# A mixture-of-experts layer: the slot-to-token table written by scatters, bias sums and zero columns without products

## The chip, the cores and the metric

The kernel runs on one core of one Trainium2 chip. TensorE (PE) multiplies, VectorE (DVE) and ScalarE (ACT) work on elements, GpSimd (POOL) and SyncE (SP) here mostly issue DMA transfers. The metric is the device time of one launch in microseconds. The kernel before takes 1660.75 us, the median of three runs (1660.35 to 1661.57).

## The reference

The input `x` holds 2 batches of 2048 tokens with 512 features, all float32. Everything that has to be computed is this:

```python
ys  = y * scale                                       # one row of 512 per batch
d   = rsqrt(einsum('bi,io->bo', ys*ys, weight*weight) + EPS)
z   = einsum('bsi,io->bso', x * ys[:, None, :], weight) * d[:, None, :]
top1    = argmax(softmax(z @ gate_w.T))               # one of two experts per token
masked  = z[None] * one_hot(top1).T[:, :, None]       # zero rows for the other expert
routed  = (relu(masked @ w1 + b1[:, None]) @ w2 + b2[:, None]).sum(over experts)
shared  = relu(z @ sw1 + sb1) @ sw2 + sb2
out = x + routed + shared
```

A token's row is zero for the expert that it did not choose, but that expert still adds `relu(b1) @ w2 + b2` to it. So each token needs its own expert's network, the constant vector of the other expert, the shared network, and three output biases in all. The hidden width is 2048.

## The kernel before, in words

The 4096 tokens are worked on in **units** of 1024 (`U`), with features on the partitions and tokens along the free axis. Four phases follow one another on TensorE:

1. `z_unit(u)` for u = 0 to 3 makes z, stores it transposed by blocks of 128 tokens in `zD` and in features-first form in `zTD`, and collects the difference of the gate's two scores per token in `score` (`rows_of`).
2. Four shared units s0 to s3 (`unit("s0")` to `unit("s3")`), in order. Each has a layer 1 of eight steps c = 0 to 7 (`layer1_once`) and a layer 2 of seven products, each made of seven smaller ones (`layer2_twice`, places m0, m2, m3, m4).
3. Three routed units r0 to r2 of 1024 tokens and one, r3, of 512, each of one expert alone, with a small group of 128 tokens beside each of the first three.
4. A last piece of 256 tokens.

Large products are made with seven instead of eight block products, so sums and differences of weight blocks have to be made on VectorE and stored. These are the split jobs (`split_twice`), spread over the shared units; they load and store through SP's queue, which also carries all weights. The constant vector of the other expert comes out of them: `zeros_add` gathers `relu(b1)` times `w2` in a tile `part`, and `zeros_end` (L388) reduces it over partitions twice by products with ones. One gives a row of 512 (L390), stored in `zeroR`; the other gives four columns of 128 (L396), stored in `zeroC`. `begin(k)` (L1545) loads the row for the small pieces (L1558) and the column for the large ones (L1555).

Between the shared units' steps runs the **sort** (`sort_parts`, L643), a generator that is advanced one part at a time by `sort_step`. From `score` it makes for each token its position in a list of 4224 slots (`pos`), ordered by expert with padding, so that each routed piece holds one expert's tokens only. The list that the rest of the kernel needs is the inverse: the token of each slot, `idx`, with 128 partitions and 33 columns (`NS`). It is made by products with 0/1 matrices: position = 128*hi + lo, and for each block c of 128 tokens VectorE compares `lo` with a row 0 to 127 (L767) and `hi` with 0 to 32, times the token's number plus one (L768); TensorE multiplies the two into one PSUM bank `pi` that collects all 32 blocks (L759). Empty slots get a padding row (L774). The tiles of the comparisons are from the ring `io` of four buffers, which the loads of x rows use too. `idx` is used by the gathers of z rows (L1562), of the stored sums (L1654) and by the scatter of the output (L1660), all indirect DMAs on GpSimd.

The order of work is written out by hand. A dictionary `hooks` names what is to be done after a step: the places `("in", c)` and `c` of layer 1, `"m0"` to `"m4"` and `("n", step, place)` of layer 2. The sort's parts run in s0 after steps 1 to 6 and at m2, m3, m4, and in s1 and s2 after steps 5 and 6 and at m2, m3, m4.

The results of a unit leave TensorE in the next one: `run_late` takes two blocks of 128 tokens after each step c = 1 to 4 of layer 1. For each it transposes the block (L1411), adds the x row that was loaded two blocks ahead (L1505, GpSimd) on VectorE (L1508), and stores the sum in `accD` (L1509, GpSimd). GpSimd's queue also carries the loads of the next unit's z (L473). Each queue keeps its order.

Of the kernel before, what the change touches and what calls it, by code (L numbers as in the profile page):

```python
# [9 lines left out]
F32 = mybir.dt.float32  # L10
I32 = mybir.dt.int32
AF = mybir.ActivationFunctionType
ALU = mybir.AluOpType
# [3 lines left out]
def kernel(  # L17
# [9 lines left out]
    sw1: bass.AP,  # L27
    sw2: bass.AP,
    b1T: bass.AP,
    b2: bass.AP,  # L30
    out: bass.AP,
):

# [31 lines left out]
    NB = N // P  # L65
    HC = H // P
    H2 = HC // 2
# [11 lines left out]
    NS = L // P  # L79
# [3 lines left out]
    add, sub = ALU.add, ALU.subtract  # L83
# [4 lines left out]
    const = ctx.enter_context(tc.tile_pool(name="const", bufs=1))  # L88
    wpool = ctx.enter_context(tc.tile_pool(name="wpool", bufs=3))
# [32 lines left out]
    w2E = dram.tile([E, H4, P, 7, 4, P], F32, name="w2E")  # L122

    zeroR = dram.tile([E, D], F32, name="zeroR")
    zeroC = dram.tile([E, P, KD], F32, name="zeroC")


    cond_sb = const.tile([P, KD, B], F32, name="cond_sb")
# [12 lines left out]
    ones = const.tile([P, P], F32, name="ones")  # L141
# [9 lines left out]
    nc.sync.dma_start(xt[0][:, :K2, T:], xT_v[:, :K2, T:U])  # L151
    nc.scalar.dma_start(xt[0][:, K2:, T:], xT_v[:, K2:, T:U])
    b1_sb = const.tile([P, E + 1, HC], F32, name="b1_sb")
    b2_sb = wpool.tile([P, D], F32, tag="w1b", name="b2_sb")
    gate_sb = wpool.tile([P, E, D], F32, tag="w1a", name="gate_sb")

    def later_loads():

        nc.scalar.dma_start(b2_sb[: E + 1, :], b2)
        load_xT(1, nc.scalar)  # L160
        nc.scalar.dma_start(gate_sb, gate.unsqueeze(0).to_broadcast([P, E, D]))
        nc.scalar.dma_start(b1_sb, b1T.rearrange("e p c -> p e c"))
# [26 lines left out]
    col_f = const.tile([P, P], F32, name="col_f")  # L189
    nc.vector.tensor_copy(col_f, col_i)  # L190

    pad_f = const.tile([P, 1], F32, name="pad_f")
    nc.vector.tensor_scalar(pad_f, tok_f[:, :1], float(N + 1), None, add)

    def sums(o, a11, a12, a21, a22):
        s1, s2, s3, s4 = o
# [33 lines left out]
    def modulation_parts():  # L230
        for k in range(KD):
            nc.scalar.activation(cw2[:, k, :], cw_sb[:, k, :], AF.Square)
        var = const.tile([P, KD, B], F32, name="var")
        pd = bank("pa", "pd")
        for k in range(KD):
            nc.tensor.matmul(pd[:B, :D], ys2[:, k, :], cw2[:, k, :], start=(k == 0), stop=(k == KD - 1))
        vr = work.tile([P, D], F32, tag="zrow", name="vr", bufs=2)
        nc.vector.tensor_scalar_add(vr[:B, :], pd[:B, :D], EPS)
        yield
        pv = bank("pa", "pv")  # L240
        for o in range(KD):
# [12 lines left out]
        yield  # L254

        pb = bank("pa", "pb")
        for o in range(KD):
            nc.tensor.matmul(
                pb[:, o : o + 1], b2_sb[: E + 1, ts(o, P)], ones[: E + 1, :1], start=True, stop=True
            )  # L260
        nc.vector.tensor_copy(bsum, pb[:, :KD])
        yield

    modulation = modulation_parts()
# [123 lines left out]
    def zeros_end(e):  # L388
        pc = bank("pa", f"pcr{e}")
        nc.tensor.matmul(pc[:1, :D], ones[:, :1], part[e], start=True, stop=True)  # L390
        row = io(f"crow{e}")
        nc.vector.tensor_copy(row[:1, :], pc[:1, :D])
        nc.gpsimd.dma_start(zeroR[1 - e].unsqueeze(0), row[:1, :])
        pc = bank("pa", f"pcc{e}")
        for o in range(KD):
            nc.tensor.matmul(pc[:, o : o + 1], part[e][:, ts(o, P)], ones[:, :1], start=True, stop=True)  # L396
        col = const.tile([P, KD], F32, name=f"ccol{e}")
        nc.vector.tensor_copy(col, pc[:, :KD])
        nc.gpsimd.dma_start(zeroC[1 - e], col)

    split_jobs = [job_w2(sw2, q, w2S[0], s2S[0], None) for q in range(H4)]
    split_jobs += [job_w1(e, q) for e in range(E) for q in range(H4)]
# [237 lines left out]
    def small(name, shape=None, dtype=F32):  # L640
        return const.tile(shape or [P, 1], dtype, name=name)

    def sort_parts():  # L643
# [101 lines left out]
        hi = small("hi", [P, NB])  # L745
        nc.vector.tensor_sub(hi, pos, lo)
        nc.vector.tensor_scalar_mul(hi, hi, 1.0 / P)
        tok1 = small("tok1", [P, NB])
        nc.vector.tensor_scalar(tok1, tok_f, 1.0, None, add)
        yield  # L750


        pi = bank("po", "pi")
        G = 4
        for c0 in range(0, NB + G, G):
            if c0 > 0:
                for i in range(G):
                    c = c0 - G + i
                    nc.tensor.matmul(  # L759
                        pi[:, :NS], at_lo[:, i], at_hi[:, i], start=(c == 0), stop=(c == NB - 1)  # L760
                    )
            if c0 < NB:
                at_lo = io(f"at_lo{c0}", [P, G, P])
                at_hi = io(f"at_hi{c0}", [P, G, NS])
                for i in range(G):
                    c = c0 + i
                    nc.vector.tensor_scalar(at_lo[:, i], col_f, lo[:, c : c + 1], None, ALU.is_equal)  # L767
                    nc.vector.tensor_scalar(  # L768
                        at_hi[:, i], col_f[:, :NS], hi[:, c : c + 1], tok1[:, c : c + 1],
                        ALU.is_equal, ALU.mult,  # L770
                    )
                yield
        none = small("none", [P, NS])
        nc.vector.tensor_scalar(none, pi[:, :NS], 0.0, pad_f, ALU.is_equal, ALU.mult)  # L774
        idx_f = small("idx_f", [P, NS])
        nc.vector.scalar_tensor_tensor(idx_f, pi[:, :NS], -1.0, none, add, add)
        idx = small("idx", [P, NS], I32)
        nc.vector.tensor_copy(idx, idx_f)
        box["idx"] = idx
        yield  # L780

# [763 lines left out]
    def begin(k):  # L1545

        ev = nc.values_load(
            box["tab"][:, k : k + 1], engines=(mybir.EngineType.SP,), min_val=0, max_val=E - 1,
            skip_runtime_bounds_check_because="a comparison's result, 0 or 1",
        )  # L1550
        b1p = work.tile([P, HC], F32, tag="b1p", name=f"b1p{k}", bufs=3)
        nc.sync.dma_start(b1p, b1T[bass.ds(ev, 1), :, :].rearrange("e p c -> p (e c)"))
        if pieces[k][1] >= T:
            zero = work.tile([P, KD], F32, tag="zc", name=f"zc{k}", bufs=2)
            nc.sync.dma_start(zero, zeroC[bass.ds(ev, 1)].rearrange("e p k -> p (e k)"))  # L1555
        else:
            zero = work.tile([P, D], F32, tag="zrow", name=f"zrow{k}", bufs=2)
            nc.sync.dma_start(zero, zeroR[bass.ds(ev, 1), :].to_broadcast([P, D]))  # L1558
        return ev, b1p, zero
# [153 lines left out]
    box["ws"] = [(w, lambda: None) for w, _ in first]  # L1713
    for u in range(NU):
        hooks = split_hooks(5, 2 if u == 0 else 1)
        if u < 3:
            when = range(1 if u == 0 else H2 - 3, H2 - 1)
            hooks = merge(hooks, {c: [sort_step] for c in [*when, "m2", "m3", "m4"]})
        if u == 0:
            hooks = merge(hooks, {  # L1720
                ("in", 0): [lambda: [rows_of(NU - 1, j) for j in range(3)]],
                0: [lambda: [rows_of(NU - 1, j) for j in range(3, 6)]],
                ("in", 1): [lambda: [rows_of(NU - 1, j) for j in range(6, U // P)]],
            })
# [112 lines left out]
```

## Time and profile before

| what | value |
|---|---|
| median of three runs | 1660.75 us (1660.35 to 1661.57) |
| the profiled execution | 1662.84 us |
| its span | 1661.1 us |
| TensorE busy | 1645.4 us, 99% |
| VectorE busy | 1109.1 us, 67% |
| ScalarE busy | 558.5 us, 34% |
| GpSimd busy | 189.9 us, 11% |
| moved by DMA | 366.07 MB, mean 220 GB/s |

The profile shows one execution. Busy times are unions of the instructions' times of one engine, so overlapping instructions count once. PE is the matmul itself, PEld its weight load, which runs beside other matmuls; a float32 matmul of the program stands as two records of each. In the order of time a row gives the start, the length, engine, line, operation and tiles, the count of merged instructions, and in square brackets the idle time before it with what ended it. L numbers are lines of the kernel before.

In time, the shared units stand as follows: s1 begins at 303 us, s2 at 493, s3 at 683, and the routed units begin at 875 us.

### The profile page before, as it was taken

The page shows a single profiled execution, that of the slowest core. Times are in us where ns is not written, and L with a number is a line of the kernel's source. Part 1 is how long each engine was busy: PE and PEld are TensorE (multiplying, and loading weights), DVE is VectorE, ACT ScalarE, POOL GpSimd, SP SyncE. Part 2 cuts the span into 40 slices and gives each one's busy share as a digit, 9 for nine tenths or more (in the row PEclk, how much of TensorE's full clock was granted, in tenths as well). Part 3 has the DMA queues.
Part 4 walks back from the last instruction along what each step waited for, and adds up shares of the span by engine and source line. Part 5 has one row for each costly group of instructions (what it writes and reads, how often), then busy time and mean ns, then how long its engine had stood idle before and what let it go on. Part 6 is the DMA issues. An engine that isn't in the chain of part 4 may idle for free. (4 is left out here: it accounts for less than half of the span.)

```text
span 1661.1 us, 19807 instructions
## 1 busy us (share of the span) xinstructions
PE 1645.4 (99%) x6786; PEld 1203.9 (72%) x6786; DVE 1109.1 (67%) x1823; ACT 558.5 (34%) x1090; POOL 189.9 (11%) x252
## 2 busy tenths in 40 slices
PE   9999999999999999999999999999999999999997
PEld 4444478645884468644888888888888888888884
DVE  5676978676877868596855588655886558874310
ACT  3334421244113331234224363243722447224210
POOL 1221000010001000011100012011110121002210
PEclk9999999999999999999999999999999999999999
DMA  5768955998578945989565665657566575544661
GB/s 180 282 238 302 361 164 175 288 351 276 165 231 287 353 145 160 301 304 332 154 208 185 236 201 185 210 180 240 188 191 209 189 237 179 164 138 143 212 229 44
DMA packets 287368, 366.07 MB, mean 220 GB/s; under 512 B 18403, under 2 KB 218595, under 8 KB 287270
## 3 DMA queue, kind: packets, MB, share of 16 engines
q1 hardware_dynamic: 263040, 287.44, 53.1%
q0 software_dynamic: 21536, 73.16, 12.4%
q10 hardware_dynamic: 2694, 4.23, 0.7%
q8 instruction: 54, 0.88, 0.2%
q14 instruction: 44, 0.36, 0.1%
HBM read 265.92 MB, written 98.84 MB: 220 GB/s over the span
## 5 line engine op out<-in xcount | busy, mean ns | idle before, releaser
L863 PE MATMUL p1s<-zs_all,was 128*128 128x512 f32 x288 | 136.0, 597 | 1.9 <-DMA was<-sw 1.9
L1312 PE MATMUL a11s<-zs_all,w2s 128*128 128x256 f32 x416 | 97.8, 379 | 0.0
L863 PEld LDWEIGHTS p1s<-zs_all,was 128*128 128x128 f32 x288 | 53.2, 190 | 60.3 <-issue 56.0
L863 PE MATMUL p1s<-zs_all,wbs 128*128 128x512 f32 x192 | 89.2, 592 | 0.0
L1312 PEld LDWEIGHTS a11s<-zs_all,w2s 128*128 128x128 f32 x416 | 78.9, 190 | 10.6
L1660 POOL DMA_INDIRECT out<-ar,idx x33 | 34.2, 1036 | 434.7 <-DVE ar L1659 414.3
L1025 PE MATMUL a11r<-tr,war 128*128 128x256 f32 x288 | 74.4, 381 | 0.3
L1312 PE MATMUL a11r<-zs_all,w2r 128*128 128x256 f32 x312 | 73.7, 379 | 0.0
L863 PEld LDWEIGHTS p1s<-zs_all,wbs 128*128 128x128 f32 x192 | 36.4, 190 | 46.1 <-issue 43.8
L1312 PEld LDWEIGHTS a11r<-zs_all,w2r 128*128 128x128 f32 x312 | 58.8, 190 | 7.7
L1025 PEld LDWEIGHTS a11r<-tr,war 128*128 128x128 f32 x288 | 54.2, 190 | 9.2 <-ACT u2r L1056 1.5
L896 DVE TENSOR_TENSOR h1s<-p5s,u3s 128x512 f32<-128x512 f32 x32 | 22.0, 689 | 47.0 <-ACT u3s L893 35.8
L1654 POOL DMA_INDIRECT ar<-accD,idx x33 | 36.5, 1106 | 147.7 <-PE pst L1572 135.3
L1312 PE MATMUL S1s<-zs_all,w2s 128*128 128x256 f32 x224 | 52.9, 379 | 0.0
L908 DVE TENSOR_TENSOR h3s<-p5s,u2s 128x512 f32<-128x512 f32 x32 | 21.9, 686 | 43.0 <-PE p5s L863 43.0
L870 ACT ACTIVATE h2s<-p1s,b_sb 128x512 f32<-128x512 f32 x32 | 22.0, 688 | 78.6 <-PE p1s L863 78.6
L1474 PEld LDWEIGHTS phr<-zp,ws 128*128 128x128 f32 x384 | 46.2, 192 | 0.9
L473 POOL DMA_DIRECT2D zs_all<-zTD x16 | 11.5, 730 | 308.6 <-PE S1s L1312 225.0
L1312 PEld LDWEIGHTS S1s<-zs_all,w2s 128*128 128x128 f32 x224 | 42.6, 190 | 5.8
L1474 PE MATMUL phr<-zp,ws 128*128 128x128 f32 x384 | 46.8, 275 | 0.0
L870 ACT ACTIVATE h0s<-p1s,b_sb 128x512 f32<-128x512 f32 x32 | 22.0, 687 | 73.5 <-PE p1s L863 73.5
L863 PE MATMUL p5s<-zs_all,was 128*128 128x512 f32 x96 | 46.2, 604 | 0.0
(484 smaller groups left out, 3839.1 us busy)
## 6 DMA issues: line engine op xcount, KB each, us to landing
ws<-w SPq DMA_DIRECT2D x48, 512.0 KB, 6.1
w2s<-w2S SPq DMA_DIRECT2D x28, 768.0 KB, 5.0
war<-w1E SPq DMA_DIRECT2D x42, 512.0 KB, 5.1
wbr<-w1E SPq DMA_DIRECT2D x42, 384.0 KB, 3.7
w2r<-w2E SPq DMA_DIRECT2D x21, 768.0 KB, 5.2
w2r<-s2E SPq DMA_DIRECT2D x20, 512.0 KB, 3.6
was<-s1S SPq DMA_DIRECT2D x24, 384.0 KB, 6.3
zTD<-zt POOLq DMA_DIRECT2D x8, 1024.0 KB, 5.2
```

The costliest lines, as they stand in the source:

```text
L473: nc.gpsimd.dma_start(zslot(slot), zTD[u][:, k : k + K2, t : t + T])
L863: nc.tensor.matmul(ps, self.w[l][:, k, :], zslot(zi, W)[:, k, :], start=(start and k == 0), stop=(k == K2 - 1), skip_group_check=not start,)
L870: nc.scalar.activation(o, i, AF.Relu, bias=bias[:, hc : hc + 1], scale=1.0)
L896: nc.vector.tensor_add(h22[:, self.c, :], self.b5, self.u3)
L908: nc.vector.tensor_add(h12[:, self.c, :], self.b5, self.u2)
L1025: nc.tensor.matmul(halves_of(ps)[:, i], w[:, i, k % 4], self.x.of[m], start=(start and i == 0), stop=True, skip_group_check=True,)
L1312: nc.tensor.matmul(ps, self.w[m][:, c, :], self.x.of[m][:, c, :], start=(start and c == 0), stop=(c == H4 - 1), skip_group_check=not start,)
L1474: nc.tensor.matmul(ph[:, ts(i, P)], w[:, k * W + i * P : k * W + (i + 1) * P], zt[:, k, :], start=(k == 0), stop=(k == KD - 1),)
L1654: nc.gpsimd.indirect_dma_start(out=ar, out_offset=None, in_=accD[:, :], in_offset=at)
L1660: nc.gpsimd.indirect_dma_start(out=out[:, :], out_offset=at, in_=ar, in_offset=None)
```

## The change

Three things are made another way.

The table `idx` is no longer a product. A table `tokD` of 4224 entries in DRAM is filled with the padding rows by one plain write, from an `idx` that starts as padding (one iota instruction). Then, for each block of 128 tokens, one indirect DMA on GpSimd writes the 128 token numbers, 4 bytes each, to their places lo*33 + hi. At the end one plain read brings the table back as `idx`. The 32 scatters are placed in layer 1 of s1 and s2, two to a step (`("in", c)` and `c`), 16 in each unit; the read is at m2 of s2. The parts of the sort ahead of that stay in s0, up to m2.

The sum of the three output biases is a reduction on VectorE over a tile that is loaded with features on the partitions, where it was four products with ones.

The zero column is not made or stored; `begin` reads the row vector of `zeroR` in column order, 4 bytes at a time.

```diff
-    zeroC = dram.tile([E, P, KD], F32, name="zeroC")
-    b2_sb = wpool.tile([P, D], F32, tag="w1b", name="b2_sb")
+    b2_sb = const.tile([P, KD, E + 1], F32, name="b2_sb")
-        nc.scalar.dma_start(b2_sb[: E + 1, :], b2)
+        nc.scalar.dma_start(b2_sb, b2T)
+    tokD = dram.tile([P * NS, 1], I32, name="tokD")
+    idx = const.tile([P, NS], I32, name="idx")
+    nc.gpsimd.iota(idx, pattern=[[0, NS]], base=N, channel_multiplier=1)
...
-        pb = bank("pa", "pb")
-        for o in range(KD):
-            nc.tensor.matmul(
-                pb[:, o : o + 1], b2_sb[: E + 1, ts(o, P)], ones[: E + 1, :1], start=True, stop=True
-            )
-        nc.vector.tensor_copy(bsum, pb[:, :KD])
+        nc.vector.reduce_sum(bsum, b2_sb, axis=mybir.AxisListType.X)
...
-        pc = bank("pa", f"pcc{e}")
-        for o in range(KD):
-            nc.tensor.matmul(pc[:, o : o + 1], part[e][:, ts(o, P)], ones[:, :1], start=True, stop=True)
-        col = const.tile([P, KD], F32, name=f"ccol{e}")
-        nc.vector.tensor_copy(col, pc[:, :KD])
-        nc.gpsimd.dma_start(zeroC[1 - e], col)
...
-        tok1 = small("tok1", [P, NB])
-        nc.vector.tensor_scalar(tok1, tok_f, 1.0, None, add)
+        at_f = small("at_f", [P, NB])
+        nc.vector.scalar_tensor_tensor(at_f, lo, float(NS), hi, ALU.mult, add)
+        at_i = small("at_i", [P, NB], I32)
+        nc.vector.tensor_copy(at_i, at_f)
+        table = tokD.rearrange("(p c) o -> p (c o)", c=NS)
+        nc.gpsimd.dma_start(table, idx)
         yield
-        pi = bank("po", "pi")
-        G = 4
-        for c0 in range(0, NB + G, G):
-            if c0 > 0:
-                for i in range(G):
-                    c = c0 - G + i
-                    nc.tensor.matmul(
-                        pi[:, :NS], at_lo[:, i], at_hi[:, i], start=(c == 0), stop=(c == NB - 1)
-                    )
-            if c0 < NB:
-                at_lo = io(f"at_lo{c0}", [P, G, P])
-                at_hi = io(f"at_hi{c0}", [P, G, NS])
-                for i in range(G):
-                    c = c0 + i
-                    nc.vector.tensor_scalar(at_lo[:, i], col_f, lo[:, c : c + 1], None, ALU.is_equal)
-                    nc.vector.tensor_scalar(
-                        at_hi[:, i], col_f[:, :NS], hi[:, c : c + 1], tok1[:, c : c + 1],
-                        ALU.is_equal, ALU.mult,
-                    )
-                yield
...
+        for c in range(NB):
+            nc.gpsimd.indirect_dma_start(
+                out=tokD[:, :], out_offset=bass.IndirectOffsetOnAxis(ap=at_i[:, c : c + 1], axis=0),
+                in_=tok_i[:, c : c + 1], in_offset=None,
+            )
+            yield
+        nc.gpsimd.dma_start(idx, table)
...
-            nc.sync.dma_start(zero, zeroC[bass.ds(ev, 1)].rearrange("e p k -> p (e k)"))
+            nc.sync.dma_start(zero, zeroR[bass.ds(ev, 1), :].rearrange("e (k p) -> p (e k)", p=P))
...
-        if u < 3:
-            when = range(1 if u == 0 else H2 - 3, H2 - 1)
-            hooks = merge(hooks, {c: [sort_step] for c in [*when, "m2", "m3", "m4"]})
+        if u == 0:
+            hooks = merge(hooks, {c: [sort_step] for c in [*range(1, H2 - 1), "m2"]})
+        elif u < 3:
+            hooks = merge(hooks, {k: [sort_step] for c in range(H2) for k in (("in", c), c)})
+        if u == 2:
+            hooks = merge(hooks, {"m2": [sort_step]})
```

More of the change, by code (lines that the diff above doesn't have):

```diff
@@ L29 @@
     b1T: bass.AP,
-    b2: bass.AP,
+    b2T: bass.AP,
     out: bass.AP,
@@ L190 @@
     nc.vector.tensor_copy(col_f, col_i)
-    pad_f = const.tile([P, 1], F32, name="pad_f")
-    nc.vector.tensor_scalar(pad_f, tok_f[:, :1], float(N + 1), None, add)
+    tokD = dram.tile([P * NS, 1], I32, name="tokD")
+    idx = const.tile([P, NS], I32, name="idx")
+    nc.gpsimd.iota(idx, pattern=[[0, NS]], base=N, channel_multiplier=1)
     def sums(o, a11, a12, a21, a22):
@@ L747, in sort_parts @@
         nc.vector.tensor_scalar_mul(hi, hi, 1.0 / P)
-        tok1 = small("tok1", [P, NB])
-        nc.vector.tensor_scalar(tok1, tok_f, 1.0, None, add)
-        yield
-        pi = bank("po", "pi")
-        G = 4
-        for c0 in range(0, NB + G, G):
-            if c0 > 0:
-                for i in range(G):
-                    c = c0 - G + i
-                    nc.tensor.matmul(
-                        pi[:, :NS], at_lo[:, i], at_hi[:, i], start=(c == 0), stop=(c == NB - 1)
-                    )
-            if c0 < NB:
-                at_lo = io(f"at_lo{c0}", [P, G, P])
-                at_hi = io(f"at_hi{c0}", [P, G, NS])
-                for i in range(G):
-                    c = c0 + i
-                    nc.vector.tensor_scalar(at_lo[:, i], col_f, lo[:, c : c + 1], None, ALU.is_equal)
-                    nc.vector.tensor_scalar(
-                        at_hi[:, i], col_f[:, :NS], hi[:, c : c + 1], tok1[:, c : c + 1],
-                        ALU.is_equal, ALU.mult,
-                    )
-                yield
[L773 to L778, printed above, removed]
+        at_f = small("at_f", [P, NB])
[4 more added lines that the diff above has]
+        nc.gpsimd.dma_start(table, idx)
+        yield
+        for c in range(NB):
[5 more added lines that the diff above has]
+        nc.gpsimd.dma_start(idx, table)
         box["idx"] = idx
@@ L1821 @@
         ("b1T", b1.reshape(E + 1, H // P, P).transpose(0, 2, 1)),
-        ("b2", b2),
+        ("b2T", rows_to_partitions(b2)),
     ]
```

## The prediction

> **What bounds the kernel now.** I read the page's engine shares and slices first, then the groups by shape, then the order of time around the instructions that go, and last the GpSimd queue, because that is where the work goes to. The span is 1661.1 us and its execution took 1662.84 us, so 1.7 us lie around the span; the median of the runs shown, 1660.75 us, is 2.1 us below that execution. I take differences from the profile and subtract them from the median.
>
> ```profile
> span 1661.1 us, 19807 instructions
> ...
> PE 1645.4 (99%) x6786; PEld 1203.9 (72%) x6786; DVE 1109.1 (67%) x1823; ACT 558.5 (34%) x1090; POOL 189.9 (11%) x252
> ...
> DMA  5768955998578945989565665657566575544661
> ```
>
> TensorE is busy 99% of the span, so a microsecond taken off it is a microsecond off the time, unless a wait opens in its place. The DMA row shows where one could: slices at 8 and 9 tenths lie in the shared units. The groups by shape (line, engine, operation, tiles, shape, count, then busy us and mean ns) show what the change takes off TensorE:
>
> ```profile
> L759 PE MATMUL pi<-at_hi,at_lo 128*128 128x33 f32 x64 | 7.8, 266 | 0.0
> ...
> L396 PE MATMUL pcc<-ones,part 128*128 128x1 f32 x16 | 2.1, 253 | 0.0
> ...
> L258 PE MATMUL pb<-ones,b_sb 3*128 3x1 f32 x8 | 1.0, 248 | 0.0
> ```
>
> The busy sums overlap at their edges, so I take starts instead. In the order of time (start, us, engine, line) one of the eight L759 groups, at the seam of units s1 and s2, is:
>
> ```profile
> 490.39 1.89 PE L1312 MATMUL a11s<-zs_all,w2s 128*128 128x256 f32 x8
> 492.12 0.98 PE L759 MATMUL pi<-at_hi,at_lo 128*128 128x33 f32 x8
> 492.93 1.96 PE L863 MATMUL p1s<-zs_all,was 128*128 128x512 f32 x4
> ```
>
> From the first product of L759 to the next useful product: 492.93 - 492.12 = 0.81 us, with no gap before or after. Does the neighbour close up when the group goes? The seam of s2 and s3 is the same code without it:
>
> ```profile
> 681.16 1.89 PE L1312 MATMUL a11s<-zs_all,w2s 128*128 128x256 f32 x8
> 682.88 1.88 PE L863 MATMUL p1s<-zs_all,was 128*128 128x512 f32 x4
> ```
>
> There the next unit begins 1.72 us after the eight records of L1312 began, their own length, and no wait follows. So the 0.81 us is really paid and nothing behind it is waiting to take its place.
>
> **What the change takes away.** (1) The 32 placement products: 8 groups of 0.81 us = 6.48 us. (2) The four bias products, L258: 28.59 us to 29.57 us, 0.98 us. The reduction that replaces them is one VectorE instruction (a reduction at L677 took 186 ns, the removed copy 161 ns) and no longer waits for TensorE. What follows on TensorE then starts 1 us earlier; its fourth product needs VectorE's L542, which ended at 31.0 us and starts earlier too, while that product moves from 33.1 to 32.1 us, so no wait opens. (3) The column products of the two zero vectors, L396: 714.00 to 714.92 us, and 771.89 to 772.80 us, together 1.83 us. Sum: 6.48 + 0.98 + 1.83 = **9.3 us**.
>
> Here a rule can be set beside the row. The Trainium skill, page "TensorE: Matmul & The Clock Gate", section "Wait — 56ns, not 53.3ns?", gives a small matmul a floor of about 25 ns from start to start, or about 62 ns where the sequencer's code handles it. By the second, 88 records (64 + 8 + 16) would cost 5.5 us, by the first 2.2 us. The row says 0.81 us for eight, about 101 ns each: each record has a 190 ns weight load of its own, and these follow one another. I use the row.
>
> VectorE loses 64 comparisons and some small ones; the comparisons start 0.2 us apart, so 13 us go. I cost that at nothing: VectorE is busy 67%, and TensorE's waits for it are already under half a microsecond. The two instructions that make the scatter's addresses are of the size of L749's (174 ns) and stand in for it.
>
> **What it adds.** In the compiled order the GpSimd queue gains one table write, 32 scatters and one read, and loses two column stores. TensorE gains nothing. Each scatter waits until the one before it has landed, and behind a waiting scatter stand, in this order, the stores of finished sums (L1509) and the loads of x rows (L1505); VectorE's L1508 waits for those loads, and behind it the sums that free TensorE's banks. In units s1 and s2 the queue holds three scatters ahead of the first stores, two for each later group of two blocks, and seven after the last group. The queue now, unit s2:
>
> ```profile
> 517.75 1.14 POOL L1509 DMA_DIRECT2D accD<-xr  x2 [23.26 <-DVE xr L1508]
> 520.35 0.54 POOL L1505 DMA_DIRECT2D xr<-x  x1 [1.45 <-DMA accD<-xr]
> 521.50 0.54 POOL L1505 DMA_DIRECT2D xr<-x  x1 [0.61 <-DMA accD<-xr]
> 530.64 1.15 POOL L1509 DMA_DIRECT2D accD<-xr  x2 [8.60 <-DVE xr L1508]
> ```
>
> One group takes 530.64 - 517.75 = 12.9 us, of which the queue works 2.2. A scatter's issue is bounded by the indirect stores L1660 (979 ns at least, 990 median, 1692 most); I take 1.0. Its landing time L has no row; the nearest is the small column store on the same queue:
>
> ```profile
> L399 POOL DMA_DIRECT2D zeroC<-ccol x2: 564/569/574, 715.6 to 773.8; - x2
> ...
> DMA to landing us min/median/max: 1.7/4.4/7.0
> ```
>
> and above it the x loads, which a scatter stands behind: 3.0 least, 5.7 median, 8.4 most. The Trainium skill speaks against this part of the change: "DMA: Bandwidth & Descriptors", section "Anatomy of one DMA — SWDGE (gpsimd) path", makes about 2.0 us of every GpSimd DMA a fixed cost, most of it the receipt of the write; a chain of 32 pays it 32 times. By that rule L is 2.0 us, by the rows 4.4 to 8.4 us. Per group the queue then needs 2.2 (stores and loads) + 1.0 + L + 1.0 = 4.2 + L: 6.2 us by the rule, 8.6 by the median, 12.6 by the longest. All are below 12.9, so the queue keeps pace. The three early scatters, at most 3 x 9.4 = 28 us, begin when the x loads are out; at seam s1 that is about 294 us (the comparisons' buffers that held those loads back until 304.7 are gone) and the first store is not due until 329.0. The seven late ones (at most 66 us) come ahead of the next unit's loads of z (L473), of which the first goes out at 631.5 us, 71 us after the last store of s2 at 560.2, and serves the seam at 683. So I cost the scatters at nothing for TensorE; if that cover is gone, see the rival below.
>
> The x loads now also go out directly behind the stores instead of after their landing, because the placement tiles no longer share their ring of four. The zero column is read from the row vector in 512 pieces of 4 bytes, four times, on the SP queue. The packet records show 9 ns for a 4-byte packet: 512 x 9 / 16 = 0.3 us; by the column load's own row it lands in 3.9 to 7.0 us. Its value is first used by L1272 at 1059.5 us, issued at 780.9, and SP's wait for the column store, 5.2 us at 775.6 us, goes or shrinks. The bias load is still 6 KB, at 10.6 us for use at 28.6. Nothing for each of these.
>
> **What stays uncertain.** One real wait for weights exists, in unit s2, in the order of time:
>
> ```profile
> 556.97 2.63 PE L863 MATMUL p1s<-zs_all,was 128*128 128x512 f32 x4 [1.91 <-DMA was<-sw]
> ```
>
> The DMA engines are full there; the window's row has stretch, length, busy PE, PEld, DVE, ACT, POOL, then clock, DMA share, GB/s:
>
> ```profile
> 540.00:560.00 20.00, 18.09 (x53) 8.65 (x52) 14.73 (x31) 7.38 (x13) 3.11 (x6) 0.95 1.03 390
> ```
>
> The wait itself is 2.1 us against the usual start-to-start, and the five slow products behind it, with the clock at 0.95 in this window, add 1.7: 3.8 us. Moved x loads can dissolve this wait or make another one. I keep it, with plus and minus 3.8.
>
> **The rivals.**
> A, the forecast: 9.3 us go, nothing replaces them: 1660.75 - 9.3 = **1651.4 us**. Its own range 1650 to 1653.5. Chance 0.62.
> B, the weight wait goes too: 1651.4 - 3.8 = 1647.6 us. For it: the x loads leave the full stretch earlier. Against: the bytes are the same. 0.12.
> C, one more such wait: 1655.2 us, two: 1659. For it: stores and loads now come in one burst of 1 MB. Against: unit s3 issues them that way already (stores at 707.62, loads at 708.76 us) and shows no such wait. 0.14.
> D, the change does not do what it says: products go, but the chains behind them (VectorE's and ScalarE's) set the pace at these seams, and half the gain stays: 1656 us. Against: the s2-s3 seam. 0.06.
> E, slower: the scatter chain backs up in s1 and s2. It begins when L exceeds 8.7 us. The queue is then late by 2(L - 8.7) when it issues the last x loads; they have 12.9 - 2.2 - 5.7 = 5.0 us to spare. Two units lose 2 x (2(L - 8.7) - 5.0), which eats the 9.3 us at L = 13.5. At L = 16 it is 19 us: 1670.6 us. Nothing the page shows on this queue for so few bytes is near it; the full DMA engines speak for it. 0.06.
>
> **How the numbers follow.** A measurement of this kernel tells about 0.2%, 3.3 us, from no change. Below 1657.4 lie A, B, D and most of C: faster 0.90. Between 1657.4 and 1664.1 lies C with two waits and the mild end of E: same 0.05. Slower 0.05. The range holds A, B, D and C with one wait and leaves out two waits and E: 1647 to 1657.5.
>
> **What would show it.** TensorE's busy time falls by 9 to 10 us to about 1636 us, with 88 fewer records, and no line waits on it for more than now. The seam at s1-s2 looks like the one at s2-s3. The scatters land in 2 to 8 us, the stores L1509 still wait for VectorE, never VectorE's L1508 for a load. A wrong prediction would show as L1508 waiting for x loads, or as TensorE waiting for weights at more places than the one in s2.

## The result and the profile after

| what | before | after |
|---|---|---|
| median | 1660.75 us (1659.34 to 1663.51, 21 runs) | 1658.47 us (1654.85 to 1660.62, 21 runs) |
| ratio of after to before | | 0.9984 [0.9977, 0.9990] |
| the profiled execution | 1662.84 us | 1657.31 us |
| its span | 1661.1 us | 1655.5 us |
| last product of TensorE ends | 1652.8 us | 1644.4 us |
| from there to the end of the span | 8.3 us | 11.1 us |

The change took off 2.3 us by the medians, 0.14%, where 9.3 us were forecast. The gain is clear of zero (the ratio's interval ends at 0.9990), but it is smaller than the 3.3 us that the prediction takes for telling a difference, and the time is 1.0 us above the upper end of its range. The removal itself went as forecast. The page of the kernel after:

```profile
span 1655.5 us, 19595 instructions
...
PE 1636.8 (99%) x6698; PEld 1194.3 (72%) x6698; DVE 1095.6 (66%) x1754; ACT 558.3 (34%) x1090; POOL 226.0 (14%) x285
...
DMA  5768955998579945898565656656566575545660
```

There are 88 records fewer and 8.6 us less of PE, where 9 to 10 were predicted. The order of time at the seam of s1 and s2 (start, us, engine, line; L1284 was L1312 and L835 was L863) shows no trace of the placement products, and nothing in their place:

```profile
486.30 1.89 PE L1284 MATMUL a11s<-zs_all,w2s 128*128 128x256 f32 x8
488.03 1.88 PE L835 MATMUL p1s<-zs_all,was 128*128 128x512 f32 x4
```

The distance is 1.73 us, that of the seam of s2 and s3 before. The gain was given back in two other places. The first is the end of the kernel. The line of the program's last instructions, L1832 before and L1807 after, has this row for GpSimd's queue (least, median and greatest duration in ns, first and last start):

```profile
L1832 POOLq DRAIN  x3: 46/109/6617, 1653.6 to 1660.8; - x3
```

and in the kernel after:

```profile
L1807 POOLq DRAIN  x3: 46/109/9132, 1645.2 to 1655.2; - x3
```

The drains stand behind an engine's last work. The longest of GpSimd's three begins as its last DMA goes out, after TensorE's last product, with no work of TensorE left that could cover it. It took 6.6 us before and takes 9.1 us now: 2.5 of the 2.8 us by which the end grew. The transfer isn't what it waits for: SyncE's wait for the landing of `out` ended 7.2 us before the end of the span in the kernel after (4.4 us before).

The second place is in s1 and s2, where TensorE waits for weights. In the order of time, at step c = 5 of layer 1 in s1, before:

```profile
365.31 1.04 PE L1411 MATMUL pos<-ident,os 128*128 128x128 f32 x8
366.19 1.88 PE L863 MATMUL p1s<-zs_all,was 128*128 128x512 f32 x4
```

and at this step of s1 and of s2, after:

```profile
363.31 1.04 PE L1383 MATMUL pos<-ident,os 128*128 128x128 f32 x8
365.24 1.95 PE L835 MATMUL p1s<-zs_all,was 128*128 128x512 f32 x4 [0.90 <-DMA was<-sw]
...
549.04 1.04 PE L1383 MATMUL pos<-ident,os 128*128 128x128 f32 x8
552.13 2.75 PE L835 MATMUL p1s<-zs_all,was 128*128 128x512 f32 x4 [2.05 <-DMA was<-sw]
554.68 2.82 PE L835 MATMUL p5s<-zs_all,was 128*128 128x512 f32 x4
```

The wait in s2 is the old one (1.91 us in the prediction's line of before); the one in s1 is not in the execution of before. To count them I add up, over s1 and s2, by how much the distance between two products exceeds the usual one; the slow products behind a long wait (2.82 us for four in place of 1.88) are in that sum. The profiled execution of before has 0 us in s1 and 3.8 in s2, that of after 1.3 and 3.8. But these are single executions, and the one of before happened to lie 2.1 us above its median, the one of after 1.2 us below. Brought to the medians (the sum plus the median less the execution, which takes it that the executions of a kernel differ in these waits alone), before has 3.8 - 2.1 = 1.7 us and after 5.1 + 1.2 = 6.3 us. So, as an estimate, the waits add 4.6 us, and the account for the medians is -9.3 + 2.8 + 4.6 = -1.9 us, against -2.3 measured.

### The profile page after: what moved, and what is told of

Same layout as the page of the kernel before. It is cut to its first block, busy times and chain, and to the rows that moved or that the text cites. A ratio compares the mean times of both kernels' runs of the same rounds, so it can differ in the third digit from the quotient of the medians.

```text
span 1655.5 us, 19595 instructions
## 1 busy us (share of the span) xinstructions
PE 1636.8 (99%) x6698; PEld 1194.3 (72%) x6698; DVE 1095.6 (66%) x1754; ACT 558.3 (34%) x1090; POOL 226.0 (14%) x285
## 5 line engine op out<-in xcount | busy, mean ns | idle before, releaser
L835 PE MATMUL p1s<-zs_all,was 128*128 128x512 f32 x288 | 135.3, 596 | 3.1 <-DMA was<-sw 2.9
L835 PEld LDWEIGHTS p1s<-zs_all,was 128*128 128x128 f32 x288 | 53.6, 190 | 64.9 <-issue 63.0
L1284 PE MATMUL a11s<-zs_all,w2s 128*128 128x256 f32 x416 | 97.8, 379 | 0.0
L835 PE MATMUL p1s<-zs_all,wbs 128*128 128x512 f32 x192 | 89.2, 592 | 0.0
L1284 PEld LDWEIGHTS a11s<-zs_all,w2s 128*128 128x128 f32 x416 | 78.9, 190 | 10.6
L1284 PE MATMUL a11r<-zs_all,w2r 128*128 128x256 f32 x312 | 73.7, 379 | 0.0
L835 PEld LDWEIGHTS p1s<-zs_all,wbs 128*128 128x128 f32 x192 | 36.4, 190 | 46.0 <-issue 44.2
L1284 PEld LDWEIGHTS a11r<-zs_all,w2r 128*128 128x128 f32 x312 | 58.8, 190 | 7.7
L1284 PE MATMUL S1s<-zs_all,w2s 128*128 128x256 f32 x224 | 52.9, 379 | 0.0
L745 POOL DMA_INDIRECT tokD<-tok_i,at_i x32 | 36.0, 1125 | 107.5 <-DMA tokD<-tok_i,at_i 98.2
L1284 PEld LDWEIGHTS S1s<-zs_all,w2s 128*128 128x128 f32 x224 | 42.6, 190 | 5.8
L835 PE MATMUL p5s<-zs_all,was 128*128 128x512 f32 x96 | 46.0, 603 | 0.0
```

Of the source, the lines that this page charges most:

```text
L745: nc.gpsimd.indirect_dma_start(out=tokD[:, :], out_offset=bass.IndirectOffsetOnAxis(ap=at_i[:, c : c + 1], axis=0), in_=tok_i[:, c : c + 1 ...
L835: nc.tensor.matmul(ps, self.w[l][:, k, :], zslot(zi, W)[:, k, :], start=(start and k == 0), stop=(k == K2 - 1), skip_group_check=not start,)
L1284: nc.tensor.matmul(ps, self.w[m][:, c, :], self.x.of[m][:, c, :], start=(start and c == 0), stop=(c == H4 - 1), skip_group_check=not start,)
```

## The experiments

Two questions: does the drain explain the end, and what of the change makes the waits? The first theory had two parts, R for the ring of four x tiles (x loads go out directly behind the stores, because the placement tiles no longer share it) and S for the scatters in the full stretch of layer 1. The rivals were N, that TensorE now comes sooner to a stretch that the DMA engines limit, and that the drain only absorbs a landing that would be waited for anyway. "Waits" below are the sums just described, in s1 and s2 of the profiled execution.

### One part alone: bias sums and zero columns

The kernel before, with only these parts of the change (the two column stores of GpSimd go with them, so 240 of its 242 DMAs are left):

```diff
...
-            nc.tensor.matmul(
-                pb[:, o : o + 1], b2_sb[: E + 1, ts(o, P)], ones[: E + 1, :1], start=True, stop=True
-            )
-        nc.vector.tensor_copy(bsum, pb[:, :KD])
+        nc.vector.reduce_sum(bsum, b2_sb, axis=mybir.AxisListType.X)
...
-            nc.tensor.matmul(pc[:, o : o + 1], part[e][:, ts(o, P)], ones[:, :1], start=True, stop=True)
...
-            nc.sync.dma_start(zero, zeroC[bass.ds(ev, 1)].rearrange("e p k -> p (e k)"))
+            nc.sync.dma_start(zero, zeroR[bass.ds(ev, 1), :].rearrange("e (k p) -> p (e k)", p=P))
```

> The kernel before with two of the three parts of the change: the bias sums and the zero columns without products; the table is still made by products, so GpSimd gets no scatter. Theory (the drain that ends GpSimd's queue grows with its indirect DMAs, and waits for weights are added in s1 and s2 by the table's part alone): the 2.8 us of the removed products come off in full, 1658.0 us, GpSimd's last drain stays at 6.6 us. Rival (every removed product in front of the DMA-bound units is given back there as a wait for weights): the 1.0 us of the bias is given back, at most 1.8 us come off, 1659 us.

1657.17 us against 1660.26 us, ratio 0.9979 [0.9972, 0.9986]: 3.1 us less, between 2.3 and 4.6. The last drain took 6.45 us, and s1 had no wait. The 24 small records are worth what their row said, 2.8 us, and these two parts give nothing back. By the floor of 62 ns in the Trainium skill ("TensorE: Matmul & The Clock Gate", "Wait — 56ns, not 53.3ns?") they would have been worth 1.5 us, which the interval leaves out.

### The ring held as it was

Two of the four tiles of the ring are taken at m4 of the unit before and given back at step 5, as the placement tiles did; no product comes back.

```diff
...
+    def hold_two():
+        for i in range(2):
+            t = io(f"hold{i}_{len(held_io)}")
+            nc.vector.memset(t[:, :1], 0.0)
+            held_io.append(t)
+    def let_go():
+        for i in range(2):
+            nc.vector.tensor_copy(seen[:, i : i + 1], held_io.pop(0)[:, :1])
...
+        if u < 2:
+            hooks = merge(hooks, {"m4": [hold_two]})
+        if 0 < u < 3:
+            hooks = merge(hooks, {5: [let_go]})
```

> The changed kernel, but two of the four buffers of the ring io are held through steps 0 to 4 of s1 and s2, as the comparison tiles held them in the kernel before, so the loads of x rows wait again for the landing of the stores. Theory R (the bunched stores and loads add the waits for weights): the added waits go, some 4 us come off against the changed kernel's 1658.5, about 1654.5 us, no wait for weights in s1. Rival S (the scatters themselves add them) and rival N (TensorE reaches a stretch that the DMA engines limit): no difference, 1658.5 us. The drain stays at 9.1 us in all.

1655.83 us, ratio 0.9972 [0.9963, 0.9981]: 4.4 us less than before, 2.1 more than the change itself took off, where theory R forecast some 4. The intervals of the two kernels are about 1.5 and 1 us wide to each side, so this gain alone is barely clear of noise. The wait in s1 is 0.2 us. In s2 its profiled execution has 6.2 us, but that execution, 1658.86 us, is nearly its slowest. The drain is 9.13 us as in the kernel after.

### The scatters moved to layer 2

They leave layer 1: in s1 and s2 one goes behind each of 16 smaller products of layer 2. `gate` makes one half of the addresses at m0, so that no scatter is issued ahead of it.

```diff
...
-            hooks = merge(hooks, {k: [sort_step] for c in range(H2) for k in (("in", c), c)})
+            hooks = merge(hooks, {"m0": [gate]})
+            places = [("n", s, n) for s in (3, 2, 5) for n in range(1, 8)][:NB // 2]
+            hooks = merge(hooks, {k: [sort_step] for k in places})
         if u == 2:
-            hooks = merge(hooks, {"m2": [sort_step]})
+            hooks = merge(hooks, {("n", 7, 7): [sort_step]})
```

> The changed kernel with all 32 scatters moved out of layer 1 into layer 2 of s1 and s2 (16 each, held back by a copy of their addresses on VectorE at m0), where the DMA engines are half idle. Theory S (scatters in the full stretch slow the weights): about 4 us come off, 1654.5 us. Rivals R and N: no difference, 1658.5 us. The drain stays at 9.1 us, as the number of indirect DMAs is the same.

1657.63 us, ratio 0.9981 [0.9972, 0.9990], 2.6 us less than before: as good as the kernel after, where theory S forecast 4 us better. The wait in s1 is still there (1.2 us), the drain too (9.13 us). So the scatters' place alone is not what costs.

### Without the scatters

This kernel leaves out the 32 table writes, so that its gathers read the padding row and its output is not the reference's. All else stays.

```diff
         for c in range(NB):
-            nc.gpsimd.indirect_dma_start(
-                out=tokD[:, :], out_offset=bass.IndirectOffsetOnAxis(ap=at_i[:, c : c + 1], axis=0),
-                in_=tok_i[:, c : c + 1], in_offset=None,
-            )
             yield
```

> The changed kernel without its 32 scatters: the table keeps its padding rows, so every gather reads padding and the output is not the reference's; all other instructions are the same. Theory (the drain grows by 79 ns for each indirect DMA): the last drain is 6.6 us again, 2.5 us come off by it, 1656.0 us if S is wrong, about 1651.5 if S is right as well. Rival (the drain's length is chance or goes with the time): it stays at 9.1 us.

1653.33 us, ratio 0.9965 [0.9952, 0.9977], 6.9 us less than before, with a last drain of 6.53 us. That lies between its two forecasts. So by the medians the 32 scatters cost 4.6 us together: 2.6 in the drain, which the rows show, and 2.0 by the difference, which is within the noise of these medians. The wait at step 5 of s1 is there without them (2.0 us in s1), so it does not need the scatters. It stands in all five executions profiled with a free ring (0.8 to 1.5 us idle), and in none of the three with two tiles held. But the ring is not its only cause: among the kernels built on the kernel before, where the placement tiles share the ring, the last one below, with 64 loads more, idles 1.0 us at the same place.

### The drain ahead of time, in the kernel before

If the last drain pays for DMAs long landed, one drain where GpSimd has nothing to do should shorten it. The edit puts one behind the last two gathers, more than 30 us ahead of GpSimd's next DMA.

```diff
-        late.append(lambda: lambda: layer2(*prev, [after(j) for j in range(n // P)]))
+        def last():
+            thens = [after(j) for j in range(n // P)]
+            nc.gpsimd.drain()
+            layer2(*prev, thens)
+        late.append(lambda: last)
```

> The kernel before with one drain instruction more in GpSimd's queue, behind the last two gathers of sums, where the queue is idle for over 30 us. Theory (GpSimd's last drain has work to do for every indirect DMA since the last drain): the drain in the middle takes 6 us or more beside TensorE's last products, the last one falls from 6.6 to about 3 us, which is what the landing of the last store takes, and 3.5 us come off: 1656.8 us. Rival (the last drain's length is fixed by what is on the chip at the end, or counts all since the start): no change, 1660.3 us.

1657.25 us, ratio 0.9982 [0.9975, 0.9989]: one instruction makes the kernel before 3.0 us faster. The rows of the new drain and of the last ones:

```profile
L1458 POOLq DRAIN  x1: 8055/8055/8055, 1613.4 to 1613.4; - x1
```

```profile
L1837 POOLq DRAIN  x3: 46/109/3112, 1652.7 to 1656.6; - x3
```

The 8.1 us now lie beside TensorE's work, and the last drain is 3.5 us shorter. A drain's row begins while DMAs ahead of it in the queue are still to be issued: 2.8 us of the new drain pass until the two gathers are out, and 1.2 us of each last drain until the last store is. The rival, that the time at the end is the landing of the last store, falls: that store stayed.

### The same drain in the kernel after

The edit is the one above.

> The changed kernel with nothing but one drain more in GpSimd's queue, behind the last two gathers of sums. Theory: the last drain falls from 9.1 to 3.1 us, 6.0 us come off the changed kernel, 1652.6 us; the waits for weights in s1 and s2 stay. Rival (drain and waits are coupled): another time.

1653.29 us, ratio 0.9960 [0.9948, 0.9971]: 7.2 us less than before, 4.9 less than the change alone. From TensorE's end to the end of the span it is now 5.0 us. The waits stay: 2.4 and 4.0 us. So the drain costs by itself, whatever the waits do.

### The ring held and the scatters in layer 2

Both edits of above, no drain.

> The changed kernel with both moves of the single tests: two buffers of the ring held as in the kernel before, and the 32 scatters in layer 2. It is the best kernel so far without its drain in the middle. Theory (the held ring and the scatters' place each take waits for weights away, the drain stays at 9.1 us): 1646.6 + 6.0 = 1652.6 us, waits in s1 and s2 under 1 us. Rival (the drain in the middle takes the waits of s2 away in some way of its own): 1655 us or more, with a wait of 2 to 6 us in s2.

1652.34 us, ratio 0.9952 [0.9939, 0.9965], 8.1 us less than before. In the order of time at the two places:

```profile
362.94 1.04 PE L1383 MATMUL pos<-ident,os 128*128 128x128 f32 x8
363.81 1.88 PE L835 MATMUL p1s<-zs_all,was 128*128 128x512 f32 x4
...
547.47 1.04 PE L1383 MATMUL pos<-ident,os 128*128 128x128 f32 x8
548.34 1.88 PE L835 MATMUL p1s<-zs_all,was 128*128 128x512 f32 x4
```

Both waits are gone: the next product begins 0.87 us after the eight small ones, their own length. The four kernels with the same drain of 9.1 us stand like this (difference of the median to the kernel before measured beside it):

| | scatters in layer 1 | scatters in layer 2 |
|---|---|---|
| ring free | -2.3 us (the change), -1.7 in its second measurement | -2.6 us |
| ring held | -4.4 us | -8.1 us |

Moving the scatters alone gains 0.3 to 0.9 us on the change, holding the ring alone 2.1 to 2.7, both together 5.8 to 6.4. The last is well clear of noise; that it is more than the sum of the other two is not, by these medians. The traces point the same way: with either move alone a wait is left in s2 (6.2 us with the ring held, 1.6 with the scatters moved), with both there is none.

### All three

> The changed kernel with three things of the experiments: two buffers of the ring held through steps 0 to 4 of s1 and s2, the scatters in layer 2, and a drain in the middle of the last piece. Theory (all of the loss is drain and added waits for weights): 1660.3 - 9.3 - 3.5 = 1647.5 us, with the usual wait of s2 left. If the drain can't be moved, 1653.5; if the waits come back in another place, up to 4 us more.

1646.62 us, ratio 0.9917 [0.9903, 0.9931]: 13.7 us less than before, the fastest of all, 11.9 below the kernel after. Its drains:

```profile
L1430 POOLq DRAIN  x1: 10572/10572/10572, 1602.4 to 1602.4; - x1
```

```profile
L1839 POOLq DRAIN  x3: 46/109/3087, 1640.7 to 1644.6; - x3
```

The account closes here: -9.3 for the products, 5.0 us at the end in place of 8.3 (-3.3), and waits of 0.9 us in place of 1.7 (-0.8) make -13.4.

### The change once more

The kernel after without an edit, measured beside the drain in the kernel before.

> The changed kernel as it is, once more, beside these runs and on the same chip. Theory (the wait in s1 comes from the free ring): a wait for weights of 1 to 2 us at step 5 of s1 again, one of 1.4 to 6 us in s2, drain 9.1 us, 1658 us. Rival (the wait in s1 was chance): none in s1.

1658.59 us, ratio 0.9987 [0.9980, 0.9993]; drain 9.13 us, waits 1.8 and 4.4 us. The result, the long drain and both waits repeat.

### What the drain counts: 64 small stores

Is it only indirect DMAs that lengthen it? Stores of 128 x 4 bytes to spare tables, 16 in a row in each shared unit, were put in the kernel before.

```diff
+    spareD = [dram.tile([P, 1], F32, name=f"spareD{i}") for i in range(8)]
+    def plain():
+        for i in range(16):
+            nc.gpsimd.dma_start(spareD[i % 8], tok_f[:, :1])
...
+        hooks = merge(hooks, {("n", 3, 4): [plain]})
```

> The kernel before with 64 small plain stores more on GpSimd's queue (128 x 4 bytes each, 16 at a time in layer 2 of every shared unit), which nothing reads. Theory (only indirect DMAs lengthen the drain): 6.6 us. Rival (every DMA of GpSimd lengthens it by 79 ns): 11.6 us.

Both sides missed: one execution took 1841.23 us, 181 us more, with a last drain of 4.09 us. The page of that run has, in the groups and among the DMA issues (count, size of each, us to landing):

```profile
L863 PE MATMUL p1s<-zs_all,was 128*128 128x512 f32 x288 | 142.5, 621 | 68.5 <-DMA was<-sw 68.5
```

```profile
spareD<-tok_f POOLq DMA_DIRECT2D x64, 0.5 KB, 27.5
```

Stores of half a KB take 27.5 us to land in the median, and TensorE waits 68.5 us for weights in this group alone. While the stores of s0 are under way, the DMA engines are busy and move next to nothing; the same window (stretch, length, busy PE, PEld, DVE, ACT and POOL, clock, DMA share, GB/s) in the kernel before and in this one:

```profile
210.00:220.00 10.00, 10.00 (x24) 4.49 (x24) 1.60 (x3) 4.40 (x8) 0.00 (x0) 1.00 1.06 318
```

```profile
210.00:220.00 10.00, 10.00 (x25) 4.43 (x24) 2.02 (x8) 4.98 (x9) 0.00 (x0) 1.00 1.22 19
```

What holds the engines was not shown, and a kernel so disturbed could not answer the question.

### 32 plain loads

Loads of 128 x 132 bytes, each behind the landing of the one before, in layer 2 of s1 and s2 of the kernel before; nothing uses what they load.

```diff
...
+    def plain():
+        nc.vector.memset(spare, 0.0)
+        for i in range(16):
+            nc.gpsimd.dma_start(spare, x[ts(i, P), :NS])
...
+        if 0 < u < 3:
+            hooks = merge(hooks, {"m0": [plain]})
```

> The kernel before with 32 small plain loads more on GpSimd's queue (128 rows of 132 bytes, one waiting for the other, 16 each in layer 2 of s1 and s2), which nothing reads. The 64 plain stores left a last drain of 4.1 us, which fits neither a drain of indirect DMAs alone (6.6) nor one that grows for good (11.6). Theory (the drain clears up what GpSimd has issued since some earlier clearing, of whatever kind, 80 ns each): 6.6 + 2.6 = 9.2 us. Rival (plain DMAs don't count or shorten it): 6.6 us or less.

1662.84 us in one execution, 1660.44 us for the kernel before beside it, and the drain

```profile
L1841 POOLq DRAIN  x3: 46/109/9145, 1651.1 to 1660.8; - x3
```

is that of 32 scatters within 20 ns. Up to this number, what counts is how many DMAs GpSimd issues, not their kind: 242 of them gave 6.5 to 6.6 us, 274 gave 9.1, in four kernels with scatters and in this one. That is 2.5 us for 32, about 80 ns each.

### 64 plain loads

The same loads in all four shared units. If the drain grows straight on, it is 11.7 us; if the short drain of the 64 stores had to do with their number, it is 4 us again.

```diff
-        if 0 < u < 3:
+        if u < 4:
             hooks = merge(hooks, {"m0": [plain]})
```

> The kernel before with 64 chained plain loads of 128 x 132 bytes on the GpSimd queue, 16 in layer 2 of each of s0 to s3, into a tile that nothing uses. The last GpSimd drain took 6.6 us with none of them, 9.1 us with 32, and 4.1 us in the kernel with 64 plain stores. Theory, the drain grows straight with the number of GpSimd DMAs: 6.6 + 64 x 0.08 = 11.7 us. Rival, something clears the account once the number passes some point between 274 and 306 DMAs: about 4 us again, as with the 64 stores, and then what counts is the DMAs since the last clearing, not their total. The time itself should stay within 6 us of the kernel before.

```profile
L1841 POOLq DRAIN  x3: 51/109/4086, 1651.8 to 1656.4; - x3
```

4.09 us, as with the stores. So the drain does not grow with the total: something seems to clear the account on the way. The order of time on GpSimd shows a candidate. Its rows end with the idle time before the DMA and what ended it; `issue` stands for a wait that the profile puts down to nothing:

```profile
807.56 0.54 POOL L1718 DMA_DIRECT2D spare<-x  x1 [4.20 <-DMA spare<-x]
813.75 0.53 POOL L1718 DMA_DIRECT2D spare<-x  x1 [5.66 <-issue]
```

The load that the second one waits for had landed at 811.1 us by the trace's semaphore records. It goes out 2.65 us later, where the others of this chain follow a landing by 0.3 us in the median. Counted from the start of the kernel, 181 DMAs of GpSimd lie ahead of that pause. Another one, of 1.8 us, stands behind the first 84. In the kernel after the place behind the first 84 falls on a scatter:

```profile
342.47 1.03 POOL L745 DMA_INDIRECT tokD<-tok_i,at_i  x1 [0.30 <-issue]
350.47 1.01 POOL L745 DMA_INDIRECT tokD<-tok_i,at_i  x1 [6.96 <-issue]
```

Most of the 6.96 us is the landing of the scatter before (at 349.1 us); the pause behind it is 1.4 us, again in place of 0.3. A pause behind 84 shows in every run whose next DMA was ready then, seven in all. The one behind 181 does not: in the kernel before and in that of 64 stores the DMA there goes out 0.3 us after the one before it, without a pause.

If the account were cleared at 84 and 181, which are 97 apart, the next place would be 278, between the 274 DMAs of the kernel after and the 306 here. Then 59, 61, 93 and 28 DMAs would remain for the last drain in the kernels with 240, 242, 274 and 306, and 1.9 us + 78 ns for each gives 6.5, 6.7, 9.2 and 4.1 us; measured are 6.45, 6.5 to 6.6, 9.1 and 4.1. That is a guess that fits, no more: two constants and three places for four lengths, no pause to be seen at 278, where GpSimd waits for other engines, and none at 181 in other kernels. After an explicit drain with two DMAs behind it the line would give 2.1 us and 2.8 to 3.1 were measured, so it doesn't hold down to the smallest counts. What is shown is that the drain gets short again somewhere between 274 and 306.

From TensorE's last product to the end of the span this kernel takes 5.8 us, 2.5 less than the kernel before. Its one execution took 1658.45 us and that of the kernel before beside it 1661.26; that says nothing, since the 21 runs of the kernel before lie 4.2 us apart.

## Why the prediction was off

**The removal sum was right.** 9.3 us for 88 records held up: the records are gone, PE is busy 8.6 us less although products behind the waits run slower, the seam closed up, unit s3 is shorter by 1.78 us (its zero columns were put at 1.83), and the bias and zero parts alone gave 3.1 us. Row against floor went to the row. The reason that was given for the row does not hold: the 190 ns weight loads cannot follow one another within 101 ns, and in the trace they start 0.11 us apart and overlap. What sets the 101 to 115 ns of a small record was not shown.

**The scatters do keep pace.** Rival E is out. They took 969 to 2007 ns to issue, 1014 in the median, where 1.0 was taken:

```profile
L745 POOL DMA_INDIRECT tokD<-tok_i,at_i x32: 969/1014/2007, 294.5 to 588.5; - x32
...
  DMA tokD<-tok_i,at_i: 98.2, 23
```

The second line is the idle time in front of scatters that waited for the one before: 98.2 us in 23 waits, 4.3 us each behind an issue of 1.0. The landing time itself, from the start of the issue, stands in the second measurement of the same kernel (`after_again`, L745):

```profile
DMA to landing us min/median/max: 2.1/5.4/9.7
```

So L was nearer to the rows (4.4 to 8.4 us) than to the 2.0 us of the Trainium skill's "Anatomy of one DMA — SWDGE (gpsimd) path" in "DMA: Bandwidth & Descriptors", which only the quickest scatters reach. L1480, which adds the x rows, has no idle time at all put down to a load, as forecast.

**The step that failed first: the sum ended at TensorE.** "A microsecond taken off it is a microsecond off the time, unless a wait opens in its place" was read from a busy share of 99%, over a span whose last 8.3 us hold no product. Nothing in the working asked what those 8.3 us are, or whether 32 more DMAs on GpSimd change them. "I cost the scatters at nothing for TensorE" was worked out from GpSimd's queue, which did keep pace, and left out the end: +2.8 us, where no engine can cover it. None of the rivals contained it. For TensorE they were not free either: with the ring held, the scatters' move out of layer 1 gained another 3.7 us.

**The step that failed second: "the x loads now also go out directly behind the stores ... Nothing".** GpSimd in s1, before (L1505 the x loads, L1509 the stores):

```profile
354.83 0.55 POOL L1509 DMA_DIRECT2D accD<-xr  x1 [5.01 <-DVE xr L1508]
356.06 0.55 POOL L1509 DMA_DIRECT2D accD<-xr  x1 [0.69 <-DVE xr L1508]
359.12 0.54 POOL L1505 DMA_DIRECT2D xr<-x  x1 [2.51 <-DMA accD<-xr]
361.68 0.54 POOL L1505 DMA_DIRECT2D xr<-x  x1 [2.02 <-DMA accD<-xr]
```

and after (L1477 and L1481):

```profile
352.83 1.17 POOL L1481 DMA_DIRECT2D accD<-xr  x2 [1.36 <-DVE xr L1480]
353.99 1.08 POOL L1477 DMA_DIRECT2D xr<-x  x2
```

Before, the loads waited for the landing of the stores and so came one by one. After, all four transfers, 1 MB, are out within 2.3 us. Rival C named this and gave it 0.14, because s3 already did so without a wait. Unit s3 was the wrong control, and its row does not tell it from s2 (stretch, length, then busy PE, PEld, DVE, ACT and POOL, clock, DMA share, GB/s; kernel after):

```profile
550.00:570.00 20.00, 17.95 (x39) 7.90 (x39) 17.39 (x40) 6.55 (x11) 4.20 (x5) 0.91 1.04 391
```

```profile
722.00:742.00 20.00, 20.00 (x60) 9.77 (x59) 18.63 (x38) 8.04 (x13) 2.90 (x6) 1.00 1.05 394
```

Both have full DMA engines, one stalls and one doesn't. Rival C with one more wait, 1655.2 us, plus the 2.8 us of the end makes 1658.0 us; measured are 1658.47. C had the mechanism of one loss, the other was in no rival, and the range did not hold both together. In the experiments, holding two tiles gave back 2.1 us, and with the scatters moved as well 5.8.

**A size: the kept wait.** The forecast held the 3.8 us of the wait in s2 constant and subtracted from the median. The median of before holds about 1.7 us of waits; the profiled execution was a long one. So rival B could never have brought 3.8 us: with the waits gone the kernel stands at -8.1 us, with 2.8 us more at its end; without those it would be -10.9, of which 9.3 are the products and only 1.6 the waits.

**What stays open.** Holding the ring alone, or moving the scatters alone, does not free s2; only both do. How the 4.6 us of waits divide between the two is within the noise. That x loads and scatters meet the weights on full DMA engines is consistent with this, but how scatters of 128 x 4 bytes lengthen a wait for weights was not shown. Nor was it shown where and why the drain's account is cleared, or tried whether the change with a few DMAs more, between 274 and 306, ends as early as with a drain.

## What to carry to other kernels

A bound of 99% says what the middle of a kernel costs; the stretch behind the last product has its own bill, and a change that adds DMAs to GpSimd has to be costed there too: read the rows of the last line's drains. If the last drain is long, put one drain of your own in a stretch where GpSimd idles; here that was worth 3.0 us in the kernel before and 4.9 us in the kernel after. And where a change frees buffers, follow which transfers go out earlier and what they collide with, and subtract from the median only what the median contains.

## What the hardware showed unasked

GpSimd's last drain takes time for DMAs that landed long ago, whether they are indirect or plain: about 80 ns for each from 242 to 274 of them (6.6 and 9.1 us). It does not grow for good: with 306 it took 4.1 us, in two kernels. Behind the first 84 DMAs the queue pauses for 1.1 to 1.9 us beyond the usual, in seven runs; whether that has to do with the drain is open. And 16 plain stores of 128 x 4 bytes in a row, up to eight of them under way at once, kept the DMA engines busy for a stretch of 10 us in which these moved 19 GB/s: four such bursts cost 181 us, while 32 scatters of the same size, each behind the landing of the last, cost about 4.6 us, the drain included.
